# The last stage of a convolution and expert kernel, rearranged image by image

## The chip, the cores and the metric

The kernel runs on one core of a Trainium2 chip. The metric is the device time of one execution in microseconds (us). A core has five engines that run side by side, each through its own queue of instructions in a fixed order: TensorE (PE: matmuls; PEld is its load of the stationary operand), VectorE (DVE), ScalarE (ACT), GpSimd (POOL) and SyncE (SP, which here only starts transfers). Engines wait for one another by semaphores. Matmul results land in PSUM, eight banks of 512 fp32 values in each of 128 partitions; everything else on the core lies in SBUF. All data here are fp32.

## The reference

Layer 0 takes x of 32 images, 128 channels, 56 by 56. It computes a 7 by 7 depthwise convolution, a layer norm over the channels, and a mixture of 8 experts with 2 per token and a limited number of places per expert; the result is `input + x_skip + layer_scale * moe`. Layer 1, which the last stage of the kernel computes, is coordinate attention and a 3 by 3 convolution:

```python
x_h = x.mean(3) + x[..., :w // 2].mean(3) + x[..., :w // 4].mean(3)
x_w = x.mean(2) + x[:, :, :h // 2].mean(2) + x[:, :, :h // 4].mean(2)
y = jnp.concatenate([x_h, x_w], axis=2)
y = jnp.einsum('ncl,mc->nml', y, w1) + b1[None, :, None]       # 128 channels to 8
y = _h_swish(_bn1d(y, g1, be1, m1, v1))
xh, xw = (y[:, :, :h], y[:, :, h:])
a_h = jax.nn.sigmoid(jnp.einsum('nml,cm->ncl', xh, wh) + bh[None, :, None])[:, :, :, None]
a_w = jax.nn.sigmoid(jnp.einsum('nml,cm->ncl', xw, ww) + bw[None, :, None])[:, :, None, :]
out = x * a_w * a_h
out = lax.conv_general_dilated(out, wc, window_strides=(1, 1), padding=[(1, 1), (1, 1)], ...)
out = (out + bc[None, :, None, None]) * s2[None, :, None, None] + (be2 - m2 * s2)[None, :, None, None]
return out * jax.nn.sigmoid(out)
```

## The kernel before

Four stages follow one another: the depthwise convolution, the layer norm and gates, the experts (whose last scatter GpSimd issues up to 3122.7 us), and layer 1. The experts leave two tables of token rows in device memory, `acc_d`: for each token one row that its first expert wrote and one that its later expert wrote. Layer 1 starts from `input + beta + first row + second row`. A row of token data is 137 values, of which 128 are read.

**Stage 4 by pairs.** The loop at the end runs over 16 pairs of images and one more turn. `load_pair` (L945) brings two images of x, 3136 KB, into `x1`. Each pair has seven `combine` steps (L950) of seven tiles of 128 tokens: two transfers of 448 KB bring the rows of both tables (`xn`, `x2`; L955), GpSimd adds them (L958), TensorE turns each tile (L964), and VectorE adds turned rows, beta and x in place, 512 columns at a time (L966). When half an image is complete, `squeeze` (L970) multiplies it by w1, four row groups side by side in the partitions of one PSUM bank (L979), and VectorE sums the result along rows and columns (L981, L982). fp32 matmuls go through TensorE in two passes, so a group of four matmuls shows as eight.

`attend` (L984) follows for a whole image: VectorE scales the sums by `wq` (L989) and adds them (L990), TensorE gathers them (L994, L997), VectorE makes the swish (L1000 to L1002), TensorE multiplies by wh and ww (L1006, L1007), and ScalarE computes both sigmoids from PSUM into SBUF tiles (L1008, L1009). VectorE then multiplies the whole image, 3136 elements per partition, by each of them (L1012, L1013): the gate. The second product goes into `pad`, which has a border of zeros.

**The convolution** works on four output rows at a time, through six combinations of six input rows, so that each needs only three horizontal taps. `attend` also makes the combinations: GpSimd and ScalarE compute `t`, `d` and `v` for the whole image at once (L1020 to L1031). `conv` (L1034) takes half an image (seven groups of four rows): six products `m[k]`, each of three taps of 392 columns into one of five PSUM banks (L1041), that is 36 passes; ScalarE copies one to `odd` (L1046), VectorE makes the first sum and difference (L1047, L1048) and adds the other products in ten steps (L1051), ScalarE applies the batch norm and silu (L1053) and starts the output (L1054). In a pair's turn the four half images of the pair before are convolved between the `combine` steps.

**The order.** The framework plans the order of each engine's instructions while the kernel is built: earlier in the program goes first, but an instruction that its own cost estimates find not yet ready lets ready ones pass. On the chip the order is then fixed. That is why the trace shows matmuls of the squeeze two or four at a time between conv passes. Sequence is also set by buffers: `x1` 2, row tiles 3, `pad` 2, `v` 2, `d` and `t` 1, `y` and `odd` 3, turned tiles 2 banks, products 5 banks, and one bank (`pa`) for the squeeze and all of the attention. The transfers of the rows wait for the 14 small VectorE clears (L854, `fence`) that follow the last scatter. SP's queue holds, in order, the loads of weights and vectors, then x and rows.

Of the kernel before, what the change touches and what calls it, by code (L numbers as in the profile page):

```python
# [38 lines left out]
VB = 2  # L39
# [8 lines left out]
def moe_conv_then_coordatt_kernel(ctx: ExitStack, tc: tile.TileContext, a: dict, out: bass.AP):  # L48
# [809 lines left out]
    with ExitStack() as st:  # L858
        cp1 = st.enter_context(tc.tile_pool(name="cc", bufs=1, reuse_waits="tile"))
        xp = st.enter_context(tc.tile_pool(name="cx", bufs=2, reuse_waits="tile"))  # L860
        kp = st.enter_context(tc.tile_pool(name="ck", bufs=3, reuse_waits="tile"))
        sp = st.enter_context(tc.tile_pool(name="cs", bufs=2, reuse_waits="tile"))
        hp = st.enter_context(tc.tile_pool(name="ch", bufs=1, reuse_waits="tile"))
        op = st.enter_context(tc.tile_pool(name="co", bufs=3, reuse_waits="tile"))
        mp = st.enter_context(tc.tile_pool(name="cm", bufs=3, reuse_waits="tile"))
        vp = st.enter_context(tc.tile_pool(name="cv", bufs=VB, reuse_waits="tile"))
        ptp = st.enter_context(tc.tile_pool(name="cpt", bufs=2, space=PSUM))
        psp = st.enter_context(tc.tile_pool(name="cps", bufs=1, space=PSUM))
        pcp = st.enter_context(tc.tile_pool(name="cpc", bufs=5, space=PSUM))
        MIP = 8  # L870
        GR = H // 4
        RP = 7
        SR = 7
        QP = 32

        def vec(name, n):
            t = cp1.tile([n, 1], F32, name=f"v_{name}")
            nc.sync.dma_start(t, a[name])
            return t

        wc = cp1.tile([C, 3, 3, C], F32, name="wc")
        nc.sync.dma_start(wc.rearrange("c h w o -> c (h w) o"), a["wc"])
        wk = [cp1.tile([C, 3, C], F32, name=f"wk{k}") for k in range(5)] + [wc[:, 2]]
        w0, w1, w2 = (wc[:, k] for k in range(3))
        nc.vector.tensor_tensor(wk[0], w0, w2, ALU.add)
        nc.vector.tensor_tensor(wk[1], wk[0], w1, ALU.add)
        nc.vector.tensor_tensor(wk[2], wk[0], w1, ALU.subtract)
        nc.vector.scalar_tensor_tensor(wk[0], w0, 0.25, w2, ALU.mult, ALU.add)  # L890
        nc.vector.scalar_tensor_tensor(wk[3], w1, 0.5, wk[0], ALU.mult, ALU.add)
        nc.vector.scalar_tensor_tensor(wk[4], w1, -0.5, wk[0], ALU.mult, ALU.add)
        for k in range(1, 5):
            nc.vector.tensor_scalar(wk[k], wk[k], 1.0 / 6.0 if k > 2 else -1.0 / 6.0, None, ALU.mult)
        nc.vector.tensor_scalar(wk[0], w0, 0.25, None, ALU.mult)

        w1t = cp1.tile([C, QP], F32, name="w1t")
        nc.gpsimd.memset(w1t, 0.0)
        nc.sync.dma_start(w1t[:, 0:MIP], a["w1"])

        quarter = [x / 56 for x in (7.0, 3.0, 1.0, 1.0)]
        wq = cp1.tile([P, 4], F32, name="wq")
        for k in range(4):
            nc.gpsimd.memset(wq[:, k : k + 1], quarter[k])
        pick = [ident[:, QP * j : QP * j + MIP] for j in range(4)]
        pick_w = [cp1.tile([P, MIP], F32, name=f"pick_w{k}") for k in range(2)]
        for k in range(2):
            nc.vector.tensor_scalar(pick_w[k], pick[0], quarter[2 * k], None, ALU.mult)
            for j in range(1, 4):
                nc.vector.scalar_tensor_tensor(pick_w[k], pick[j], quarter[2 * k + j // 2], pick_w[k], ALU.mult, ALU.add)  # L910
        wht = cp1.tile([MIP, C], F32, name="wht")
        nc.sync.dma_start(wht, a["wh"])
        wwt = cp1.tile([MIP, C], F32, name="wwt")
        nc.sync.dma_start(wwt, a["ww"])
        for t in (wht, wwt):
            nc.vector.tensor_scalar(t, t, 1.0 / 6.0, None, ALU.mult)
        bh, bw = vec("bh", C), vec("bw", C)

        def folded(g, be, mean, v, b, n):

            vg, vb, vm, vv, vbias = (vec(x, n) for x in (g, be, mean, v, b))
            s = cp1.tile([n, 1], F32, name=f"s_{g}")
            o = cp1.tile([n, 1], F32, name=f"o_{g}")
            mh = cp1.tile([n, 1], F32, name=f"mh_{g}")
            nc.gpsimd.memset(mh, -0.5)
            nc.vector.tensor_scalar(s, vv, 1e-5, None, ALU.add)
            nc.gpsimd.tensor_tensor(s, s, mh, ALU.pow)
            nc.vector.tensor_tensor(s, s, vg, ALU.mult)
            nc.vector.tensor_tensor(o, vbias, vm, ALU.subtract)
            nc.vector.tensor_tensor(o, o, s, ALU.mult)  # L930
            nc.vector.tensor_tensor(o, o, vb, ALU.add)
            return s, o

        s1, o1 = folded("g1", "be1", "m1", "v1", "b1m", MIP)
        s2, o2 = folded("g2", "be2", "m2", "v2", "bc", C)

        pads = []
        for k in range(2):
            t = cp1.tile([C, H + 2, W + 2], F32, name=f"pad{k}")
            nc.gpsimd.memset(t, 0.0)  # L940
            pads.append(t)
        QT = 7
        L = H + W

        def load_pair(i):  # L945
            x1 = xp.tile([C, 2, HW], F32, tag="x1", name=f"x1_{i}")
            nc.sync.dma_start(x1, a["x"][2 * i : 2 * i + 2].rearrange("n c h w -> c n (h w)"))
            return x1

        def combine(i, q, x1):  # L950
            j0 = i * TPP + q * QT
            xn = kp.tile([P, QT, C], F32, tag="cxn", name=f"cxn{i}_{q}")
            x2 = kp.tile([P, QT, C], F32, tag="cx2", name=f"cx2{i}_{q}")
            for t, r0 in ((xn, j0 * P), (x2, T1 + j0 * P)):
                d = nc.sync.dma_start(t, acc_d[r0 : r0 + QT * P, 0:C].rearrange("(j p) c -> p j c", p=P))  # L955
                for x in fence:
                    after(d.ins, x)
            nc.gpsimd.tensor_tensor(xn, xn, x2, ALU.add)  # L958
            xf = x1.rearrange("c n f -> c (n f)")
            for g in range(0, QT, 4):  # L960
                n = min(4, QT - g)
                pt = ptp.tile([C, 4 * P], F32, tag="pt", name=f"cpt{i}_{q}_{g}")
                for j in range(n):
                    nc.tensor.transpose(pt[:, j * P : (j + 1) * P], xn[:, g + j, :], ident)  # L964
                cols = slice((q * QT + g) * P, (q * QT + g + n) * P)
                nc.vector.scalar_tensor_tensor(xf[:, cols], pt[:, 0 : n * P], beta_c, xf[:, cols], ALU.add, ALU.add)  # L966

        sums = {}

        def squeeze(i, im, half, x1):  # L970

            if half == 0:
                sums[i, im] = (psp.tile([P, SR * W + L], F32, tag="pa", name=f"cpa{i}_{im}"),
                               sp.tile([P, 2, SR, 4], F32, tag="rs", name=f"rs{i}_{im}"),
                               sp.tile([P, 2, W], F32, tag="cs", name=f"cs{i}_{im}"))
            pa, rs, cs = sums[i, im]
            for j in range(4):
                f0 = (4 * half + j) * SR * W
                nc.tensor.matmul(pa[j * QP : (j + 1) * QP, 0 : SR * W], lhsT=w1t, rhs=x1[:, im, f0 : f0 + SR * W],  # L979
                                 start=True, stop=True)  # L980
            nc.vector.tensor_reduce(rs[:, half], pa[:, 0 : SR * W].rearrange("p (r q v) -> p r q v", r=SR, q=4), AX.X, ALU.add)  # L981
            nc.vector.tensor_reduce(cs[:, half, :], pa[:, 0 : SR * W].rearrange("p (r w) -> p w r", r=SR), AX.X, ALU.add)  # L982

        def attend(i, im, x1):  # L984
            img = x1[:, im, :].rearrange("c (h w) -> c h w", h=H)
            nm = f"{i}_{im}"
            pa, rs, cs = sums.pop((i, im))
            ry = sp.tile([P, 2, SR], F32, tag="ry", name=f"ry{nm}")
            nc.vector.tensor_tensor(rs, rs, bc(wq.unsqueeze(1).unsqueeze(1), [P, 2, SR, 4]), ALU.mult)  # L989
            nc.vector.tensor_reduce(ry, rs, AX.X, ALU.add)  # L990
            pl = pa[:, SR * W : SR * W + L]
            py = pl[0:MIP, :]
            for j in range(4):
                nc.tensor.matmul(py[:, 0:H].rearrange("m (k j r) -> m k j r", k=2, j=4)[:, :, j, :], lhsT=pick[j], rhs=ry,  # L994
                                 start=True, stop=True)
# [63 lines left out]
        for i in range(NPAIR + 1):  # L1059
# [3 lines left out]
            for q in range(NQ):  # L1063
# [9 lines left out]
                for x in todo[: per_q[q]]:  # L1073
                    conv(*x)
# [61 lines left out]
```

## Time and profile before

| | us |
|---|---|
| time, median of 3 runs (lowest, highest) | 4329.18 (4310.08, 4334.66) |
| the profiled execution's time | 4323.54 |
| its span | 4321.8 |
| stage 4 in the span, from the first setup of it | about 3123 to the end, 1199 |
| PE, DVE, ACT, POOL busy in it | 1079, 971, 361, 934 |

The profile is of one execution; its parts used here are windows (busy time of each engine in a stretch), groups of instructions by line, waits (who waited for whom), the timeline, and the chain of work that ended last. A busy DVE or POOL instruction includes time for which it stood inside the engine and could not move. `PEclk`, the granted TensorE clock, is 1.00 in nearly all of stage 4 after 3300 us and 0.50 to 0.53 between 3123 and 3150.

### The profile page before, as it was taken

What the parts mean: (1) busy time and instruction counts of PE and PEld (TensorE: products, weight loads), DVE (VectorE), ACT (ScalarE), POOL (GpSimd) and SP (SyncE); (2) the same over time, 40 slices, a digit from 0 to 9 for tenths busy, and PEclk for the clock granted to TensorE, in tenths of its full rate; (3) what the DMA queues carried; (4) which work ended last, traced back from release to release, by engine and by line L of the source; (5) the groups of instructions that cost most, each with busy time, mean ns of one, the idle gap of its engine ahead of it and who ended that gap; (6) DMA issues with size and microseconds to landing.
All of it is one profiled execution on the core that took longest, in us unless ns stands there. A gap on an engine that the chain in (4) does not pass through costs nothing. (4 is left out here: it accounts for less than half of the span.)

```text
span 4321.8 us, 60777 instructions
## 1 busy us (share of the span) xinstructions
PE 3526.6 (82%) x21765; PEld 2018.7 (47%) x21765; DVE 2571.0 (59%) x5370; ACT 1447.6 (33%) x3123; POOL 2752.9 (64%) x2044
## 2 busy tenths in 40 slices
PE   7999979884169858778688668989669999999999
PEld 4555559884134434444344334434334444454444
DVE  4333329999748648775622112222268888888886
ACT  0000027664034424334344334545312333333332
POOL 5444414333057777576777467777779877788875
PEclk9999989786579879889799889999879999999999
DMA  9999985553982121111222122222265555555551
GB/s 183 179 186 191 188 179 222 245 239 166 327 267 51 51 61 43 48 44 49 54 56 56 45 59 57 56 56 57 60 226 163 193 182 176 166 192 182 184 163 73
DMA packets 678005, 580.92 MB, mean 134 GB/s; under 512 B 405848, under 2 KB 611184, under 8 KB 667248
## 3 DMA queue, kind: packets, MB, share of 16 engines
q1 hardware_dynamic: 411408, 319.81, 25.7%
q10 hardware_dynamic: 222816, 160.70, 14.1%
q0 software_dynamic: 43264, 94.64, 8.1%
q8 instruction: 187, 3.06, 0.3%
q14 instruction: 330, 2.70, 0.2%
HBM read 314.92 MB, written 260.09 MB: 133 GB/s over the span
## 5 line engine op out<-in xcount | busy, mean ns | idle before, releaser
L702 POOL DMA_INDIRECT acc_d<-yo,row x676 | 685.7, 1014 | 274.9 <-DMA acc_d<-yo,row 70.4
L1041 PE MATMUL pc<-v,wk 128*128 128x392 f32 x1920 | 705.5, 510 | 0.4 <-POOL v L1026 0.4
L661 PE MATMUL ph<-fxt,w 128*128 128x512 f32 (+1 forms) x1400 | 682.5, 631 | 0.5 <-ACT ht L662 0.5
L640 POOL DMA_INDIRECT xg_r<-acc_d,idx x556 | 557.4, 1003 | 183.9 <-issue 108.5
L669 PE MATMUL py<-ht,w 128*128 128x512 f32 (+1 forms) x1400 | 624.6, 589 | 0.0
L165 PE MATMUL acc<-xs,band 28*64 28x432 f32 (+2 forms) x11264 | 536.1, 527 | 51.8 <-issue 33.0
L662 ACT ACTIVATE ht<-ph,bias 128x512 f32<-128x512 f32 (+1 forms) x700 | 476.8, 682 | 248.9 <-PE ph L661 246.4
L1041 PEld LDWEIGHTS pc<-v,wk 128*128 128x128 f32 x1920 | 348.2, 191 | 308.5 <-issue 104.9
L165 PEld LDWEIGHTS acc<-xs,band 28*64 28x64 f32 x11264 | 311.2, 132 | 276.1 <-issue 182.9
L310 PE MATMUL lnps<-proj,lnyt 128*128 128x136 f32 x1568 | 364.7, 401 | 67.4 <-ACT sq L315 38.8
L661 PEld LDWEIGHTS ph<-fxt,w 128*128 128x128 f32 x1400 | 274.1, 207 | 279.3 <-issue 250.9
L310 PEld LDWEIGHTS lnps<-proj,lnyt 128*128 128x128 f32 x1568 | 350.9, 316 | 81.7 <-ACT sq L315 47.9
L669 PEld LDWEIGHTS py<-ht,w 128*128 128x128 f32 x1400 | 254.6, 190 | 261.1 <-issue 259.2
L1051 DVE SCALAR_TENSOR_TENSOR y<-pc,y 128x392 f32<-128x392 f32 x640 | 317.3, 553 | 14.9 <-PE pc L1041 14.9
L1021 POOL TENSOR_TENSOR d<-pad 128x3248 f32<-128x3248 f32 x32 | 228.0, 7125 | 151.8 <-DVE pad L1013 151.8
L958 POOL TENSOR_TENSOR cxn<-cxn,cx 128x896 f32<-128x896 f32 x112 | 267.3, 2395 | 75.6 <-DMA cxn<-acc_d 28.8
L696 DVE TENSOR_TENSOR ys<-pb,xg_r 128x512 f32<-128x512 f32 (+2 forms) x147 | 98.3, 671 | 341.3 <-PE pb L678 341.1
L181 DVE TENSOR_TENSOR yt<-acc,m 128x448 f32<-128x448 f32 x256 | 146.4, 620 | 260.3 <-PE acc L165 188.3
L671 ACT ACTIVATE fyt<-py,b 128x512 f32<-128x512 f32 (+1 forms) x175 | 119.6, 683 | 507.0 <-PE py L669 496.7
L653 DVE COPY fxt<-pt 128x512 f32<-128x512 f32 (+1 forms) x175 | 119.5, 683 | 241.7 <-PE pt L651 238.7
L693 ACT ACTIVATE yo<-xg_r,own 128x137 f32<-128x137 f32 (+1 forms) x568 | 194.3, 404 | 191.1 <-DVE own L689 128.3
L331 DVE SCALAR_TENSOR_TENSOR xn<-cen,rstd,gamma_bc 128x128 f32<-128x128 f32 x784 | 213.5, 340 | 47.2 <-POOL rstd L324 47.2
(243 smaller groups left out, 5035.4 us busy)
## 6 DMA issues: line engine op xcount, KB each, us to landing
acc_d<-xn SPq DMA_DIRECT2D x16, 3356.5 KB
acc_d<-yo ACTq DMA_DIRECT2D x4, 13426.0 KB
lnyt<-y_d SPq DMA_DIRECT2D x16, 3136.0 KB
x<-in_x SPq DMA_DIRECT2D x16, 3136.0 KB
cxn<-acc_d SPq DMA_DIRECT2D x112, 448.0 KB
cx<-acc_d SPq DMA_DIRECT2D x112, 448.0 KB
out<-y ACTq DMA_DIRECT2D x64, 784.0 KB
xt<-in_x ACTq DMA_DIRECT2D x64, 392.0 KB
```

The costliest lines, as they stand in the source:

```text
L165: nc.tensor.matmul(acc[r][half * M : (half + 1) * M, :, lo:hi], lhsT=band[rows, t0 + o - least, 1 - par : 1 - par + M], rhs=xs[i][rows, ha ...
L310: nc.tensor.matmul(ps[:, j, :], lhsT=yf[:, self.j0 + g + j, :], rhs=proj, start=True, stop=True)
L331: nc.vector.scalar_tensor_tensor(pair.row[:, self.j0 + j, 0:C], self.cen[:, j, 0:C], self.rstd[:, j : j + 1], gamma_bc, ALU.mult, ALU.mult)
L640: d = nc.gpsimd.indirect_dma_start(out=xg[0:n, k, :], out_offset=None, in_=acc_d[0:T1, :], in_offset=bass.IndirectOffsetOnAxis(ap=idx[0][0 ...
L661: nc.tensor.matmul(ph[:, 0:N_], lhsT=w[0][:, f * P : (f + 1) * P], rhs=xt[:, 0:N_], start=True, stop=True)
L662: nc.scalar.activation(ht[:, f, 0:N_], ph[:, 0:N_], AF.Gelu, bias=w[2][:, f : f + 1])
L669: nc.tensor.matmul(py[:, 0:N_], lhsT=w2[:, f, :], rhs=ht[:, f, 0:N_], start=(f == 0), stop=(f == NF - 1))
L702: d = nc.gpsimd.indirect_dma_start(out=acc_d[:, :], out_offset=bass.IndirectOffsetOnAxis(ap=row[0:n, k : k + 1], axis=0), in_=yo[0:n, k, : ...
L958: nc.gpsimd.tensor_tensor(xn, xn, x2, ALU.add)
L1021: nc.gpsimd.tensor_tensor(d, high, low, ALU.subtract)
L1041: nc.tensor.matmul(m[k], lhsT=wk[k][:, dw, :], rhs=v[:, k, rows, dw : dw + W], start=(dw == 0), stop=(dw == 2))
L1051: nc.vector.scalar_tensor_tensor(r[x], m[k], f, r[y_], ALU.mult, ALU.add)
```

## The change

Stage 4 goes image by image. Rows come in blocks of eight image rows, seven to an image: 448 tokens as four tiles of 112 (`load_rows`), with x in blocks too (`load_x`), eight blocks ahead. GpSimd adds the second table's rows to the first's (`summed`), four blocks ahead; TensorE turns the four tiles and VectorE writes the merged block straight into the padded image (`merge`), which is gated in place. The sigmoids are written back to PSUM, `wq` is copied there once, and the swish starts from PSUM, so no VectorE step of the loop reads two SBUF tensors. The combinations are made for half an image at a time, in two parts (`combined`); `d`, `t`, `v` and `y` hold half an image. Each image has a slot of pieces in a written order (`slots`): in the first half of slot k the blocks of image k are merged between the conv pieces of the second half of image k-2; in the second half image k is attended and gated between the conv pieces of the first half of image k-1. There are 34 slots. Constants load through ScalarE's queue, and the borders of `pad` alone are cleared, by VectorE. The planner works as before. The setup of the weights is left out here, as it computes the same values.

Of the removed lines, which the listing above has, none is repeated here.

```diff
+    trp = ctx.enter_context(tc.tile_pool(name="ctr", bufs=2, space=PSUM))
+    pcp = ctx.enter_context(tc.tile_pool(name="cpc", bufs=5, space=PSUM))
...
+    MB = 8
+    NM = H // MB
+    MT = 2 * W
+    NX = 8
...
+    xss = [cp1.tile([C, MB, W], F32, name=f"xs{k}") for k in range(NX)]
+    cxs = [[cp1.tile([MT, BLK, C], F32, name=f"cx{i}_{k}") for i in range(2)] for k in range(NX)]
+    def load_x(m):
+        nc.sync.dma_start(xss[m % NX], a["x"][m // NM][:, m % NM * MB : (m % NM + 1) * MB, :])
+    def load_rows(m):
+    ys = [cp1.tile([C, RP, 4, W], F32, name=f"y{k}") for k in range(2)]
+    odd = cp1.tile([C, RP, W], F32, name="odd")
+    pads = [cp1.tile([C, H + 2, W + 2], F32, name=f"pad{k}") for k in range(2)]
+    vs = [cp1.tile([C, 6, RP, W + 2], F32, name=f"v{k}") for k in range(2)]
+    d_t = cp1.tile([C, RP, 4, W + 2], F32, name="d_t")
+    t_t = cp1.tile([C, RP, 2, W + 2], F32, name="t_t")
...
+    pa = psp.tile([P, SR * W + L + 8], F32, name="pa")
...
+    wq_ps = pa[:, SR * W + L : SR * W + L + 4]
+    nc.vector.tensor_copy(wq_ps, wq)
...
+    for t in pads:
+        nc.vector.memset(t[:, 0 : H + 2 : H + 1, :], 0.0)
+        nc.vector.memset(t[:, :, 0 : W + 2 : W + 1], 0.0)
+    def summed(m):
+        if m < NM * N:
+            x, x2 = cxs[m % NX]
+            nc.gpsimd.tensor_tensor(x, x, x2, ALU.add)
+    def merge(k, q):
+        m = NM * k + q
+        pt = trp.tile([P, BLK * P], F32, tag="tr", name=f"cpt{k}_{q}")[:, 0 : BLK * MT]
+        for j in range(BLK):
+            nc.tensor.transpose(pt[:, j * MT : (j + 1) * MT], cxs[m % NX][0][:, j, :], ident[0:MT, 0:MT])
+        nc.vector.scalar_tensor_tensor(pads[k % 2][:, 1 + q * MB : 1 + (q + 1) * MB, 1 : W + 1],
+                                       pt.rearrange("c (r w) -> c r w", w=W), beta_c, xss[m % NX], ALU.add, ALU.add)
+        if m + NX < NM * N:
+            load_x(m + NX)
+            load_rows(m + NX)
+        summed(m + 4)
+    def squeeze(n, half):
+        pad = pads[n % 2]
+        for j in range(4):
+            r0 = 1 + (4 * half + j) * SR
+            nc.tensor.matmul(pa[j * QP : (j + 1) * QP, 0 : SR * W], lhsT=w1t, rhs=pad[:, r0 : r0 + SR, 1 : W + 1],
+                             start=True, stop=True)
+        nc.vector.tensor_reduce(rs[:, half], pa[:, 0 : SR * W].rearrange("p (r q v) -> p r q v", r=SR, q=4), AX.X, ALU.add)
+        nc.vector.tensor_reduce(cs[:, half, :], pa[:, 0 : SR * W].rearrange("p (r w) -> p w r", r=SR), AX.X, ALU.add)
+    pl = pa[:, SR * W : SR * W + L]
+    def pooled(n):
+        nc.vector.tensor_tensor(rs, rs, bc(wq_ps.unsqueeze(1).unsqueeze(1), [P, 2, SR, 4]), ALU.mult)
+        nc.vector.tensor_reduce(ry, rs, AX.X, ALU.add)
+        py = pl[0:MIP, :]
+        for j in range(4):
+            nc.tensor.matmul(py[:, 0:H].rearrange("m (k j r) -> m k j r", k=2, j=4)[:, :, j, :], lhsT=pick[j], rhs=ry,
+                             start=True, stop=True)
         for k in range(2):
+            nc.tensor.matmul(py[:, H:L], lhsT=pick_w[k], rhs=cs[:, k, :], start=(k == 0), stop=(k == 1))
+        nc.vector.tensor_scalar(py, py, s1, o1, ALU.mult, ALU.add)
+        nc.vector.tensor_scalar(r_t, py, 3.0, 0.0, ALU.add, ALU.max)
+        nc.vector.scalar_tensor_tensor(z_t, r_t, 6.0, py, ALU.min, ALU.mult)
+    def attend(n):
+        ph, pw = pl[:, 0:H], pl[:, H:L]
+        nc.tensor.matmul(ph, lhsT=wht, rhs=z_t[:, 0:H], start=True, stop=True)
+        nc.tensor.matmul(pw, lhsT=wwt, rhs=z_t[:, H:L], start=True, stop=True)
+        nc.scalar.activation(ph, ph, AF.Sigmoid, bias=bh)
+        nc.scalar.activation(pw, pw, AF.Sigmoid, bias=bw)
+    def gate(n):
+        img = pads[n % 2][:, 1 : H + 1, 1 : W + 1]
+        nc.vector.tensor_tensor(img, img, bc(pl[:, H:L].unsqueeze(1), [C, H, W]), ALU.mult)
+        nc.vector.tensor_tensor(img, img, bc(pl[:, 0:H].unsqueeze(2), [C, H, W]), ALU.mult)
+    def combined(n, ch, part):
+        v, pad = vs[ch], pads[n % 2]
+        r0 = 4 * RP * ch
+        byq = lambda x: x.rearrange("c (g r) w -> c g r w", r=4)
+        low, high = byq(pad[:, r0 : r0 + 4 * RP, :]), byq(pad[:, r0 + 2 : r0 + 2 + 4 * RP, :])
+        d, t = d_t, t_t
+        if part == 0:
             nc.scalar.mul(t, low[:, :, 1:3, :], 4.0)
             nc.gpsimd.tensor_tensor(d, high, low, ALU.subtract)
             nc.gpsimd.tensor_tensor(t, high[:, :, 1:3, :], t, ALU.subtract)
             nc.gpsimd.tensor_tensor(v[:, 1], t[:, :, 1, :], t[:, :, 0, :], ALU.add)
             nc.gpsimd.tensor_tensor(v[:, 2], t[:, :, 1, :], t[:, :, 0, :], ALU.subtract)
+        else:
+            nc.scalar.mul(v[:, 3], d[:, :, 1, :], 2.0)
+            nc.scalar.mul(d[:, :, 0:2, :], d[:, :, 0:2, :], 4.0)
+            nc.gpsimd.tensor_tensor(v[:, 4], d[:, :, 2, :], v[:, 3], ALU.subtract)
+            nc.gpsimd.tensor_tensor(v[:, 3], d[:, :, 2, :], v[:, 3], ALU.add)
             nc.gpsimd.tensor_tensor(v[:, 0], d[:, :, 2, :], d[:, :, 0, :], ALU.subtract)
             nc.gpsimd.tensor_tensor(v[:, 5], d[:, :, 3, :], d[:, :, 1, :], ALU.subtract)
+    PASSES = {3: ((2, 0, 4.0), (3, 1, 8.0), (0, 0, 1.0), (1, 1, 2.0)),
+              4: ((0, 0, 1.0), (1, 1, -2.0), (2, 2, 4.0), (3, 3, -8.0)), 0: ((0, 0, 1.0),), 5: ((3, 3, 1.0),)}
+    def product(n, ch, k):
+        m = pcp.tile([P, RP, W], F32, tag="pc", name=f"pc{n}_{ch}_{k}")
+        for dw in range(3):
+            nc.tensor.matmul(m, lhsT=wk[k][:, dw, :], rhs=vs[ch][:, k, :, dw : dw + W], start=(dw == 0), stop=(dw == 2))
+        return m
+    def conv(n, ch, ks):
+        y = ys[ch]
+        r = [y[:, :, k, :] for k in range(4)]
+        m = {k: product(n, ch, k) for k in ks}
+        if 1 in m:
             nc.scalar.copy(odd, m[1])
             nc.vector.tensor_tensor(r[0], m[2], odd, ALU.add)
             nc.vector.tensor_tensor(r[1], odd, m[2], ALU.subtract)
+        for k in ks:
+            for x, y_, f in PASSES.get(k, ()):
                 nc.vector.scalar_tensor_tensor(r[x], m[k], f, r[y_], ALU.mult, ALU.add)
+        if 5 in m:
             yf = y.rearrange("c r t w -> c (r t) w")
             nc.scalar.activation(yf, yf, AF.Silu, bias=o2, scale=s2)
+            nc.scalar.dma_start(out[n][:, 4 * ch * RP : 4 * (ch + 1) * RP, :], yf)
+    def slots(k):
+        new = lambda f, *x: (lambda: f(*x)) if k < N else None
+        old = lambda d, f, *x: (lambda: f(k - d, *x)) if 0 <= k - d < N else None
+        cv = lambda *ks: old(2, conv, 1, ks)
+        pieces = [new(merge, k, 0), cv(1, 2), old(1, combined, 0, 1), new(merge, k, 1), new(merge, k, 2), cv(3),
+                  new(merge, k, 3), new(squeeze, k, 0), cv(4), new(merge, k, 4), new(merge, k, 5), cv(0), new(merge, k, 6),
+                  new(squeeze, k, 1), cv(5)]
+        cv = lambda *ks: old(1, conv, 0, ks)
+        pieces += [old(1, combined, 1, 0), new(pooled, k), cv(1, 2), new(attend, k), old(1, combined, 1, 1), cv(3),
+                   new(gate, k), cv(4), cv(0), cv(5), new(combined, k, 0, 0)]
+        return [f for f in pieces if f]
+    for m in range(4):
+        summed(m)
+    for k in range(N + 2):
+        for f in slots(k):
+            f()
```

## The prediction

> **What bounds the kernel now.** The change touches only the last stage, so I read the page's 40 slices first to place it (about 3123 us to the end, 1199 of the 4321.8 us span), then windows of one pair of images each, then the waits of TensorE, then the timeline around one gate. Windows of two steady pairs (columns: length, then busy time of PE, PEld, DVE, ACT, POOL, then granted clock, DMA share, GB/s):
>
> ```profile
> 3867.00:3938.00 71.00, 66.92 (x259) 34.99 (x258) 60.63 (x85) 22.79 (x22) 58.29 (x24) 1.00 0.57 184
> 3938.00:4009.00 71.00, 66.83 (x259) 34.75 (x258) 60.62 (x86) 22.79 (x22) 58.33 (x25) 1.00 0.57 182
> ```
>
> TensorE is idle only 4.1 us per pair, 2.05 us per image; VectorE and GpSimd have 10 and 13 us idle per pair. What TensorE waits for in 3797 to 4080 us (eight images; total, times, longest):
>
> ```profile
> PE cpa L994 <- DVE ry L990: 7.5, 7, 1.2
> PE cpa L1006 <- DVE z L1002: 7.2, 8, 1.0
> ```
>
> Both are small VectorE steps of the attention. The timeline shows the same steps first with GpSimd idle or between instructions, and then in the steady state:
>
> ```profile
> 3157.96 0.21 DVE L989 TENSOR_TENSOR rs<-rs,wq 128x56 f32<-128x56 f32 x1
> 3160.43 0.26 DVE L1002 SCALAR_TENSOR_TENSOR z<-r,z 8x112 f32<-8x112 f32 x1
> 3167.12 3.41 DVE L1013 TENSOR_TENSOR pad<-x,ah 128x3136 f32<-128x3136 f32 x1
> ...
> 3871.31 2.06 DVE L1002 SCALAR_TENSOR_TENSOR z<-r,z 8x112 f32<-8x112 f32 x1
> 3873.29 1.97 DVE L1051 SCALAR_TENSOR_TENSOR y<-pc,y 128x392 f32<-128x392 f32 x4
> 3879.00 4.83 DVE L1013 TENSOR_TENSOR pad<-x,ah 128x3136 f32<-128x3136 f32 x1
> ...
> 3902.97 1.89 DVE L989 TENSOR_TENSOR rs<-rs,wq 128x56 f32<-128x56 f32 x1
> 3911.46 4.39 POOL L958 TENSOR_TENSOR cxn<-cxn,cx 128x896 f32<-128x896 f32 x1 [2.91 <-issue]
> ```
>
> Steps with two SBUF inputs wait for a GpSimd step, and hold one up (4.39 us where it took 2.08 alone). Steps with one input in PSUM (L1051) stay at 0.49 us, and GpSimd's L1021, beside them, at 7.10 to 7.16 us. Period: the gates of image 0 and of image 30 end at 3170.5 and 4237.1 us, 35.55 us per image; an undisturbed pair takes 70.6, 35.3 per image. The end, from the chain of work (start, length):
>
> ```profile
> 4261.56 53.55 PE pc L1041 x162
> 4315.13 0.58 DVE y L1051
> 4315.73 1.69 ACT y L1053
> ```
>
> After the last gate TensorE alone decides (0.331 us per pass), then 4.4 us of output.
>
> **The change part by part, per image.**
>
> *VectorE.* The scaling of the row sums falls from 1.65 (by-form mean) to 0.21, the swish from 1.79 to 0.26, the gate from 3.55 + 4.69 to 3.40 + 3.41. Now: 20 accumulating steps at 0.49 = 9.8, 4 first ones at 0.5 = 2.0, seven merges of 448 elements (512 take 0.635 pipelined, so 0.57) = 4.0, four reductions 2.1, small ones 1.4, gate 6.8: 26.1 us, against 60.6/2 = 30.3. It is not the bound; this frees 4 us that decide nothing by themselves.
>
> *TensorE.* Conv passes are the same 72. Transposes go from 24.5 to 28; seven take 0.77, so 3.5 x 0.11 = +0.4. Squeeze: 16 passes in both, but now all four of a half are issued together. Eight passes in a row took 1.39 us, two alone 0.78; the chain's pieces of one pair add to 8.4, so 4.2 per image now and 2.8 if both halves stay together: -1.4, or 0 where the planner pulls them apart as it does now; I take -0.7. Busy 33.25 - 0.7 + 0.4 = 32.95. The idle 2.05 goes: the picks and the attention's matmuls are now followed or preceded by ready conv pieces (cv(5), cv(1, 2)), and the VectorE step ahead of them is 0.2 and not 1.9 us.
>
> *GpSimd.* 64 differences of 1624 elements (7.12/2 = 3.56) 7.1 per image, the t steps 3.1, v1 and v2 3.3, v3 and v4 3.55, v0 and v5 3.85; the row sums are seven of 512 elements on 112 partitions, 2.08 x 512/896 = 1.19 each = 8.3 (7.3 before, uncontended). With about 0.05 us for each of 12 more instructions: 29.8 us. It was 28.1 uncontended, 29.2 with its stalls. This is 90% of a period of 33; what is late next, if anything, is here.
>
> *The wait that is added.* GpSimd's row sums run only four blocks ahead, and its first-half pieces of image k stand in its queue behind gate(k). From gate(k) to the last row sum of image k+1 GpSimd does difference, t, v1, v2 (6.8), v4, v3, v0, v5 of the half (3.6), three sums (3.6): 14.0. From there to the end of gate(k+1): transposes 0.45, merge 0.57, squeeze 1.4, reductions 1.04, scaling 0.45, picks 0.6, swish 0.9, matmuls 0.6, sigmoids 0.8, gate 6.8 = 13.6, plus 4.7 for the conv products and accumulations that stand ahead on TensorE and VectorE (cv(5) and cv(1, 2) partly) = 18.3. The ring takes 32.3 us, just under TensorE's 32.95. Queued behind gate(k) on VectorE are cv(4), cv(0), cv(5); TensorE has five product banks to run on, 10 us, and the gate takes 6.8. Period: 32.95 + 0.35 for remaining waits = 33.3; ends 31.9 (squeezes together, no wait) and 35.3 (nothing gained).
>
> *ScalarE.* One sigmoid and one swish table load per image as now (8 and 8 in eight images); 11.4 us of work per image, covered by a period of 33.
>
> *Buffers.* y has one per half image (three before): its output must land before cv(1, 2) of that half a slot later, some 16 us after issue; at the end it takes 4.4. odd has one: its two readers run 16 us before the next copy. Sigmoids stay in the bank that the squeeze writes: squeeze(k, 0) waits for gate(k-1), which ends about 3 us into the slot, the squeeze stands 8 us into it. None is on the path.
>
> *Transfers.* SP issues 21 per image instead of 7.5; an issue is 0.36 to 0.52 us, 10 us per image, in a queue that otherwise waits. Bytes are the same 6.4 MB per image: at 182 GB/s 35.2 us, at the 426 GB/s of the busiest window (3923 to 3927) 15. Since DMA is at share 0.57, I take it as hidden; the cover gone, it is the first rival below. The Trainium skill speaks against smaller transfers: SBUF — State Buffer, The DMA setup-cost knee, gives each about 2 us fixed plus bytes at 436 GB/s. One after the other, 21 of 229 KB would be an estimated 53 us per image, and the end at some 4815 us. The rows here show several 448 KB transfers in flight at 316 to 426 GB/s for 12 us on end, so I go by bytes.
>
> *Front.* SP no longer issues 13 small loads ahead of the data (3122.89 to 3128.9), and two 2.9 us clears leave GpSimd. The rows become readable at 3124.8, when VectorE's fence is through. First sum at about 3129.5 (two issues 1.0, 458 KB at 361 GB/s 1.3, 2.3 to land, as the scatters' transfers before it took; it was 3142.66, behind a 3136 KB load), seven sums at 1.27 each (458 KB at 361 GB/s, just over GpSimd's 1.19): 3138.4. With the 13.6 us chain and 3 more for a granted clock that stood at 0.50 there, gate(0) ends at 3155, between 3150 and 3165; now 3170.5. VectorE's set-up, 10 us in 3124.7 to 3136.7 now, ends before the seventh merge. Image 1 has few conv pieces beside it: 29 us (14.0 + 13.6 and little else).
>
> *End.* After gate(31) three half images are left, 36 passes of 0.331 = 11.9 us each, less 2 already begun: 33.7. GpSimd needs 20.8 for both halves of image 31, so TensorE decides. With 0.6 + 1.7 + 4.4: 40.4 us, 39 to 45. Now it is 51.7 (that gate ends at 4270.1).
>
> **Sum.** 3155 + 29 + 30 x 33.3 + 40.4 = 4223.4 us of span, -98.4 against the profiled 4321.8 (15.5 at the front, 71.6 between the first and last gate, 11.3 at the end). That execution took 4323.54, 0.13% under the median of 4329.18; the same difference from the median gives 4231. Own range 4182 (gate(0) at 3150, period 31.9, end 39: 4175 of span) to 4296 (gate(0) at 3165, 35, end 45: 4289).
>
> **Rivals.**
> Transfers: smaller pieces come late, GpSimd's sum stands at the head of its queue waiting for rows, and the period stays at 35.3. For it: the loads bunch in the first half, 4.8 MB in some 16 us, 300 GB/s. Against: 361 and 399 GB/s at the front. 3155 + 29 + 1059 + 40.4 = 4283.4, a time of 4291. Chance 0.10.
> The change doesn't do what it says: PSUM operands don't free the steps. Then 2 us idle stay, period 35.3, again 4291. Against: L1051 and L966, one operand in PSUM, never stretch. Chance 0.06.
> Slower: the ring through GpSimd. If all of cv(5), cv(1, 2), cv(3) and the latter's accumulations come ahead of the gate, the second part is 13.6 + 2.0 + 4.1 + 2.0 + 2.0 = 23.7 and the period 37.7: 4355.4 of span, 4363. It decides from a period of 36.6 (1097.4/30), a second part of 22.6. For it: program order is just this, GpSimd runs at 90%, sums only four blocks ahead, and waits in the middle of its queue for the gate. Against: the planner takes ready work first, as the split squeezes of now show. Chance 0.19, a quarter of it near 36.6, so within 0.5%.
>
> **How the numbers follow.** Forecast 0.65, rivals 0.10, 0.06, 0.19. A measurement here can tell about 0.5%, 22 us. Faster by more: the forecast and most of the first two, 0.77. Within: 0.07. Slower: 0.16. The range holds the forecast's own, both 4291 cases and the ring's lighter half: 4190 to 4340, leaving out about 0.05 below and 0.13 above.
>
> **What would show it.** In steady windows: scaling and swish under 0.4 us, both gate steps near 3.4 in every image, GpSimd's differences near 3.6; sigmoid table loads 33.3 us apart; TensorE busy 32 to 33 of it. Wrong if TensorE's transposes wait for GpSimd's sums by over 3 us per image, if the sums wait for DMA, or if the gate takes more than 7.5 us. The front is right if the first sum starts before 3132, the end if the last sigmoid is 45 to 55 us from the end (gate included).

## The result, and the profile after

The changed kernel takes 4361.81 us (median of 4; 4355.74 to 4375.92), the kernel before beside it 4323.16 (median of 4; 4310.08 to 4334.66): ratio 1.0104, 95% interval 1.0079 to 1.0129. It is slower by 1.0%; 4231 us and a gain of 2.3% were forecast. The profiled execution took 4355.74 with a span of 4354.0. One run further down, of the kernel with PSUM undone, fell in a slower state of the chip and is left out of its median.

The ends of the stage came as forecast, the middle did not. The gate of image 0 ends at 3151.7 us (forecast 3155), image 1 follows after 28.8 (29), and from the end of the last gate, 4314.3, it is 39.8 us to the end (40.4). Between the gates of image 1 and image 31 lie 1133.7 us, 37.8 per image, where 33.3 were forecast and 35.5 had been. 30 x 4.5 = 135 us; less the 3 us by which the front came early, that is the whole error of 131.

Windows of the kernel after (length, then busy time of PE, PEld, DVE, ACT, POOL, then clock, DMA share, GB/s); the third is the last image, when no more rows are to be summed or loaded:

```profile
3870.00:3941.00 71.00, 64.86 (x238) 33.76 (x238) 45.65 (x73) 23.24 (x28) 59.23 (x46) 0.93 0.64 175
3941.00:4012.00 71.00, 65.41 (x242) 33.52 (x241) 45.63 (x80) 22.20 (x27) 59.00 (x46) 0.93 0.60 164
4277.00:4311.00 34.00, 34.00 (x135) 17.66 (x134) 26.02 (x44) 11.79 (x14) 21.72 (x16) 1.00 0.12 48
```

VectorE has lost 15 us of work per 71 us, as the change says. No engine is full, TensorE is idle 6 us in 71 (it was 4), and its clock is at 0.93 where it was 1.00. In the last image it never stops. The waits of 3500 to 4200 us, some 18.5 images (total, times, longest):

```profile
ACT v L1035 <- POOL d_t L1030: 268.4, 35, 11.4
DVE y L1058 <- ACT odd L1057: 77.9, 19, 6.2
POOL cx L971 <- DMA cx<-acc_d: 75.3, 19, 5.3
PE pa L1011 <- DVE z_t L1007: 48.8, 19, 4.7
```

TensorE waits for the swish (L1007), which on VectorE stands behind the first sum of a half image (L1058), which waits for ScalarE's copy `odd`; and GpSimd's row sums (L971) wait for rows. The chain of work joins these. One turn of it (start, length; the pieces between are left out where "..." stands):

```profile
3888.86 0.38 ACT odd L1057
...
3889.26 0.57 DVE y L1058
...
3890.81 0.27 DVE z_t L1007
...
3891.12 0.67 PE pa L1011 x2
3891.79 0.43 PE pa L1012 x2
3892.22 8.15 PE pc L1048 x18
3900.36 0.40 PE cpt L977 x4
...
3901.80 1.28 POOL cx L971
3903.10 0.33 SPq L886
...
3903.52 3.14 DMA cx<-acc_d
...
3906.80 1.26 POOL cx L971
3908.06 3.59 POOL d_t L1030
...
3920.01 3.63 POOL d_t L1030
...
3923.66 0.55 ACT v L1035
...
3925.03 1.68 ACT y L1065
3926.71 0.38 ACT odd L1057
```

From `odd` to the next `odd` it is 37.85 us, the period. The gate is not in this chain: it ended at 3901.4 and GpSimd began the difference `d` of the gated image only at 3908.0. GpSimd's own timeline shows why:

```profile
3901.80 1.27 POOL L971 TENSOR_TENSOR cx<-cx,cx 112x512 f32<-112x512 f32 x1 [3.83 <-issue]
3906.79 1.27 POOL L971 TENSOR_TENSOR cx<-cx,cx 112x512 f32<-112x512 f32 x1 [3.72 <-DMA cx<-acc_d]
3908.02 3.63 POOL L1030 TENSOR_TENSOR d_t<-pad 128x1624 f32<-128x1624 f32 x1
```

Two sums stand ahead of `d` and wait 3.8 us each for rows. They are the sums of blocks of the image after next, some 35 us ahead of the transposes that need them. The program writes a sum four blocks ahead; the planner, which lets ready work pass, had moved it ahead, in front of `d`; by its rule it must have held the rows to be there and `d` to be still waiting for the gate.

SP's queue has a part in these waits that is easily overlooked. A load of the second table waits for the sum that frees its buffer, and every load behind it in SP's queue waits too. In the chain above the rows for the second sum leave right after such a load, which SP could issue only when the first sum was done (3903.10). SP's waits of 3500 to 4200:

```profile
SPq L886 <- POOL cx L971: 513.8, 110, 10.1
```

How much of the loss is due to SP's order alone was not tested.

### The profile page after: what moved, and what is told of

Its sections match the earlier page's. It is cut to its first block, busy times and chain, and to the rows that moved or that the text cites. A ratio compares the mean times of both kernels' runs of the same rounds, so it can differ in the third digit from the quotient of the medians.

```text
span 4354.0 us, 62611 instructions
## 1 busy us (share of the span) xinstructions
PE 3584.1 (82%) x21877; PEld 2046.6 (47%) x21877; DVE 2432.2 (56%) x5381; ACT 1458.1 (33%) x3219; POOL 2779.6 (64%) x2405
## 5 line engine op out<-in xcount | busy, mean ns | idle before, releaser
L1048 PE MATMUL pc<-v,wk 128*128 128x392 f32 x2304 | 884.0, 525 | 5.8 <-POOL v L1032 4.8
L702 POOL DMA_INDIRECT acc_d<-yo,row x676 | 685.1, 1014 | 265.9 <-issue 80.5
L1048 PEld LDWEIGHTS pc<-v,wk 128*128 128x128 f32 x2304 | 431.2, 199 | 361.6 <-issue 133.7
L971 POOL TENSOR_TENSOR cx<-cx,cx 112x512 f32<-112x512 f32 x224 | 284.0, 1274 | 231.7 <-DMA cx<-acc_d 131.1
L1030 POOL TENSOR_TENSOR d_t<-pad 128x1624 f32<-128x1624 f32 x64 | 232.4, 3632 | 15.9 <-DVE pad L1019 15.7
```

The costliest lines, as they stand in the source:

```text
L702: d = nc.gpsimd.indirect_dma_start(out=acc_d[:, :], out_offset=bass.IndirectOffsetOnAxis(ap=row[0:n, k : k + 1], axis=0), in_=yo[0:n, k, : ...
L971: nc.gpsimd.tensor_tensor(x, x, x2, ALU.add)
L1030: nc.gpsimd.tensor_tensor(d, high, low, ALU.subtract)
L1048: nc.tensor.matmul(m, lhsT=wk[k][:, dw, :], rhs=vs[ch][:, k, :, dw : dw + W], start=(dw == 0), stop=(dw == 2))
```

## Experiments

Chips differ: on some, the stages ahead of this one take 560 us more. So each run has its difference (of the medians) to the kernel before, on the same chip and in the same rounds, its ratio with a 95% interval, which is not the quotient of these medians, and the period, from gate to gate, from its own profile. A ring is a closed chain of waits through several engines, from a step of one image to the same step of the next; the longest ring sets the period. The changed kernel, run once more so, is 33.5 us above before (ratio 1.0081, 1.0044 to 1.0118), where 40 to 50 were expected.

> The changed kernel again, on the chip of the runs below, so that they can be set against it and not only against the kernel before: 40 to 50 us above before, 38 us from gate to gate.

**Sums where they are written.** An ordering edge on GpSimd's queue, that waits for nothing (`behind`), keeps each sum behind `last`, the last step of a `combined` part written ahead of it.

```diff
-            nc.gpsimd.tensor_tensor(x, x, x2, ALU.add)
+            s = nc.gpsimd.tensor_tensor(x, x, x2, ALU.add)
+            if last:
+                behind(s.ins, last[0])
...
```

> The change as it is, but GpSimd's row sums stay behind the combination steps ahead of which the program writes them (ordering edges on GpSimd's own queue, no new wait). Theory A, GpSimd's queue closes the ring: in the changed kernel two sums stand ahead of the difference d of the gated image and wait 3.8 us each for rows; here d starts within 1 us of the gate's end (it was 6.6 us), and the 36 to 38 us from gate to gate become 33.5 to 34.5: 28 images x 4 us less than 4362, so 4250, between 4230 and 4290. Theory B, ScalarE's queue closes it (the copy odd stands behind v3 of the second half): under 1% less, 4320 to 4362. Theory C, the ring written in the prediction (conv products and accumulations ahead of the gate): no change, 4340 to 4365.

+46.8 us, ratio 1.0096 (1.0058 to 1.0134): no gain, theory A fails as it was put. The two waits are gone, `d` starts 0.1 us after the gate, yet the period stays, 37.65 us, the same in nearly every image. GpSimd and ScalarE of this run:

```profile
4437.90 3.64 POOL L1038 TENSOR_TENSOR d_t<-pad 128x1624 f32<-128x1624 f32 x1 [7.25 <-DVE pad L1027]
...
4449.93 7.41 POOL L977 TENSOR_TENSOR cx<-cx,cx 112x512 f32<-112x512 f32 x6
4457.31 3.61 POOL L1038 TENSOR_TENSOR d_t<-pad 128x1624 f32<-128x1624 f32 x1
```

```profile
4460.95 0.54 ACT L1043 ACTIVATE v<-d_t 128x406 f32<-128x406 f32 x1 [14.14 <-POOL d_t L1038]
...
4462.32 1.68 ACT L1073 ACTIVATE y<-y,o_g,s_g 128x1568 f32<-128x1568 f32 x1
4463.90 0.46 ACT L1065 COPY odd<-pc 128x392 f32<-128x392 f32 x1
```

Seven sums, six of them in a row, now lie between the two `d` of an image, and ScalarE stands 14.14 us at the head of its queue with `v3 = 2 d1` of the second half, with the silu and `odd` behind it. From the gate's end (4437.8) over `d`, sums, `d`, `v3`, silu, `odd`, swish, sigmoids to the next gate's end (4475.4): 37.65 us. The work that was ahead of the gate is behind it, in the same ring.

**The copy `odd` on VectorE.**

```diff
-            nc.scalar.copy(odd, m[1])
+            nc.vector.tensor_copy(odd, m[1])
```

> The change as it is, but VectorE makes the copy odd of the first product, not ScalarE. Theory B: VectorE's wait for odd, 77.9 us in 19 images (4.1 each), goes, the swish behind it comes as much earlier, TensorE's wait for z (about 5 us per image) goes, and the period falls from 38 to 34: 4362 - 28 x 4 = 4250, between 4230 and 4290. Theory A: the link through ScalarE is only one of the ring's, d still stands behind two sums that wait for rows; under 1.5% less, 4300 to 4362. Theory C: no change.

+47.7 us, ratio 1.0093 (1.0068 to 1.0118), period about 38: no gain here either; VectorE's wait for `odd` and TensorE's for the swish are gone, but GpSimd waits 62.1 us in 16 sums for rows, 3.9 each, and the sigmoids stand behind the start of an output, which waits for a transfer of rows.

**Both edits.**

> Both edits, sums in their written order and the copy odd on VectorE. A and B: TensorE's own work decides, 33 to 33.7 us per image: 3152 + 29 + 30 x 33.4 + 40 = 4223, between 4205 and 4250. Theory C: 4330 to 4365.

-35.0 us, ratio 0.9924 (0.9900 to 0.9948), period 34.59: together they gain 82 us over either alone, but miss the number. The chain of this run, of GpSimd and ScalarE alone between two gates:

```profile
4415.00 0.90 POOL d_t L1038
...
4427.05 2.79 POOL cx L977 x3
...
4430.70 2.49 POOL cx L977 x2
4433.18 3.58 POOL d_t L1038
...
4436.79 0.55 ACT v L1043
...
4438.15 1.69 ACT y L1073
...
4440.28 1.28 ACT L1021
```

The swish is no longer behind `v3`, but the sigmoids (L1021) still are, and the sums are between the two `d`.

**Sums six ahead.** As the run before, with the sums written six blocks ahead.

```diff
-        summed(m + 4)
+        summed(m + 6)
...
```

> Row sums in written order, but written six blocks ahead and not four, and the copy odd on VectorE. With four ahead the period was 34.59 with GpSimd busy from the gate's end to the last sum: that is the ring of the prediction (gate, combinations, sums, transposes, squeeze, gate). If so, two more sums ahead take 2.5 us out of it and TensorE decides: 33.0 to 33.9 us per image, and the first gap falls from 34.0 to about 29: 25 to 50 us below the run with four ahead, 60 to 85 below before. If it is TensorE itself that needs 34.6 (finer pieces, 33.9 us busy): the period stays, only the first gap gains, 5 us. If sums at six ahead wait for rows: over 34.6.

-75.4 us, ratio 0.9827 (0.9791 to 0.9863), period 33.69. Windows of the two (with four ahead, then with six):

```profile
4400.00:4700.00 300.00, 293.69 (x1150) 151.98 (x1146) 236.63 (x385) 97.64 (x108) 260.64 (x199) 1.00 0.70 183
```

```profile
3600.00:4000.00 400.00, 400.00 (x1570) 208.46 (x1570) 320.44 (x525) 128.95 (x143) 358.58 (x272) 1.00 0.73 191
```

The number came, not for the reason given: the ring at 34.59 was not the prediction's (sums, transposes, squeeze), but the one in the chain above. Of the five sums ahead of the second `d` three stay (3.71 us), `d` and `v3` come earlier, and TensorE works without a pause, through transfers at 191 GB/s. What stays is TensorE's own work, 33.69 us.

**The order alone.** `odd` stays on ScalarE, and `v3` of the second half is put behind it (`copied`, the latest one) in ScalarE's queue; sums six ahead.

```diff
-            nc.scalar.mul(v[:, 3], d[:, :, 1, :], 2.0)
+            twice = nc.scalar.mul(v[:, 3], d[:, :, 1, :], 2.0)
+            if ch == 1:
+                behind(twice.ins, copied[0])
...
```

> As the run before with sums six ahead, but the copy odd stays on ScalarE, and v3 of the second half is put behind it in ScalarE's queue: no work changes its engine, only the order. If the place in the queue was the matter and not the work: within 15 us of the run with odd on VectorE, a period under 34.5. If ScalarE's work itself is the matter, or if v3 behind odd comes too late for GpSimd: 36 to 38 us per image, 70 us or more above it.

-93.8 us, ratio 0.9805 (0.9753 to 0.9857), period 33.69; a second time, on another occasion, -80.5 (0.9853, 0.9819 to 0.9887). TensorE works without a pause here too:

```profile
3600.00:4000.00 400.00, 400.00 (x1570) 207.85 (x1569) 305.96 (x502) 139.27 (x168) 359.50 (x272) 1.00 0.68 193
```

No work has left its engine: the places of the sums and of `v3` in two queues were the whole loss of the change, and what it was to gain comes out. This version beats both kernels. Two parts of it were not run by themselves: sums six ahead without the move of `v3`, and that move with the sums four ahead.

> The repaired order once more, on the chip of the other three runs: 33.69 us per image, 85 to 100 us below before.

**No sums.** The row sums are left out; the second table's rows are loaded, but are missing from the result.

```diff
-            nc.gpsimd.tensor_tensor(x, x, x2, ALU.add)
+            pass
```

> The changed kernel without GpSimd's row sums (the second table's rows are loaded, but left out of the result). Two rings of nearly one length (one through ScalarE's queue, 37.65 us in the run with the sums in written order, one through sums that wait for rows, 38 us in the run with odd on VectorE), both through GpSimd: both lose the sums, 7.4 us of GpSimd's work between d of the first half and d of the second, and the waits for rows. Then TensorE decides: 33 to 34 us per image, 4.3 x 29 = 125 us below the changed kernel, 70 to 90 below before. Rival, the ring through ScalarE does not hold the sums: 36 to 38 us stay, at most 50 below the changed kernel.

-48.9 us (0.9882, 0.9837 to 0.9926), less than the 70 to 90 that were expected. From image 12 on 33.74 us, with TensorE full; images 3 to 11 take 34 to 40. In these the loads of the second table, which nothing holds up any more, run far ahead (DMA share 1.17, 270 GB/s from 3280 to 3500, later 0.46). So the expectation on the sums holds where the transfers are quiet; the run also takes a quarter of the traffic out there (143 GB/s, against 191 in the run with six ahead), and doesn't tell sums from transfers. The run with six ahead does, as it has all of both.

**Which wait for rows closes the second ring.** Two places were left open: the two sums ahead of `d`, and the start of the output ahead of the sigmoids. The start is put behind the sigmoids, once with `odd` on VectorE, once in the changed kernel as it is.

```diff
-            nc.scalar.dma_start(out[n][:, 4 * ch * RP : 4 * (ch + 1) * RP, :], yf)
+            start = lambda: nc.scalar.dma_start(out[n][:, 4 * ch * RP : 4 * (ch + 1) * RP, :], yf)
+            if ch == 1 and n + 2 < N:
+                held.append(start)
+            else:
+                start()
...
-        nc.scalar.activation(pw, pw, AF.Sigmoid, bias=bw)
+        sig = nc.scalar.activation(pw, pw, AF.Sigmoid, bias=bw)
+        while held:
+            tc.add_manual_dep(held.pop()().ins, sig.ins.name,
+                              mybir.DependencyInfo(mybir.DependencyClass.NoSync, mybir.DependencyReason.DATA),
+                              reason="the output starts behind the sigmoids")
```

> The run with odd on VectorE (38 us per image, sums where the planner put them), and the start of the second half's output is put behind the sigmoids in ScalarE's queue. If that start, which waits for a transfer of rows with the sigmoids behind it, closes the second ring: the period falls from 38 to 34.5 or less, 4381 less 28 x 3.6 = 4280, 50 to 75 us below before. If the two sums ahead of d, 3.8 us of wait each, close it: 37 to 38 stays, 30 to 50 above before. If both: 35 to 37.

+59.6 us (1.0127, 1.0087 to 1.0166), period 38.7, a little above the 37 to 38 that were expected if the two sums decide: the start of the output is not what does. The chain of waits of this run goes round through the sums:

```profile
4454.51 3.34 DVE pad L1025
4457.85 0.34 SPq L881
...
4458.29 4.59 DMA cx<-acc_d
...
4462.92 0.09 issue
4463.01 1.28 POOL cx L971
4464.31 0.33 SPq L886
...
4464.73 3.38 DMA cx<-acc_d
...
4468.25 1.26 POOL cx L971
4469.51 3.58 POOL d_t L1036
```

After the gate SP issues a load of x that had been waiting in its queue, then the rows behind it; they arrive 4.6 us later, the sum, another load, 3.4 us, the second sum, and only then `d`: 11.6 us between the end of the gate and the beginning of `d`, with no work on GpSimd but 2.5 us of sums.

> The changed kernel with that edit alone (odd stays on ScalarE). The ring through odd was 37.65 without any wait for rows, so it stays: 37.5 to 38.3 us per image, within 20 us of the changed kernel. If the start of the output alone made the loss: 34.5, 100 us below it.

+70.2 us (1.0157, 1.0111 to 1.0203), 39 to 40 us per image: no gain, as expected, and a little worse than that.

**The operands in PSUM alone,** in the kernel before: sigmoids, `wq` and the swish's input in the squeeze's bank, which is one tile for all images; nothing else.

```diff
-            nc.vector.tensor_tensor(rs, rs, bc(wq.unsqueeze(1).unsqueeze(1), [P, 2, SR, 4]), ALU.mult)
+            nc.vector.tensor_tensor(rs, rs, bc(wq_ps.unsqueeze(1).unsqueeze(1), [P, 2, SR, 4]), ALU.mult)
...
-            nc.vector.scalar_tensor_tensor(z, r, 6.0, z, ALU.min, ALU.mult)
+            nc.vector.scalar_tensor_tensor(z, r, 6.0, py, ALU.min, ALU.mult)
...
-            nc.scalar.activation(ah, ph, AF.Sigmoid, bias=bh)
+            nc.scalar.activation(ph, ph, AF.Sigmoid, bias=bh)
...
-            nc.vector.tensor_tensor(img, img, bc(aw.unsqueeze(1), [C, H, W]), ALU.mult)
+            nc.vector.tensor_tensor(img, img, bc(pw.unsqueeze(1), [C, H, W]), ALU.mult)
```

> The kernel before with one part of the change alone: sigmoids, scaling weights and swish in PSUM, so that its VectorE steps there have one SBUF input. If those slow steps alone made TensorE's 2.05 us idle per image: the gate takes 3.4 + 3.4, scaling and swish under 0.3, 4323 - 31 x 2 = 4261, between 4250 and 4290. If another wait takes their place (GpSimd's or a transfer's): within 0.5% of 4323.

-73.2 us (0.9834, 0.9792 to 0.9876), and -88.4 (0.9846, 0.9787 to 0.9905) the second time. Two gates take 66.04 us, 33.02 per image, where it was 35.3. Windows and VectorE's groups of it (mean ns of one):

```profile
4400.00:4700.00 300.00, 300.00 (x1162) 157.92 (x1162) 231.93 (x381) 103.14 (x100) 253.84 (x106) 1.00 0.59 190
```

```profile
L1014 DVE TENSOR_TENSOR pad<-x,pa 128x3136 f32<-128x3136 f32 x9 | 30.7, 3412 | 0.0
...
L992 DVE TENSOR_TENSOR rs<-rs,pa 128x56 f32<-128x56 f32 x9 | 1.8, 203 | 0.0
```

Steps with two SBUF inputs were all that TensorE was waiting for, and no new wait took their place. The run frees the gate along with the two small steps. That it was the scaling and the swish rests on the waits before: those behind them were 14.7 us of some 16 that TensorE was idle in eight images.

> The kernel before with the operands in PSUM alone, on the same chip: 33.0 us per image, 65 to 80 us below before. It should stand 10 to 30 us above the repaired order, which has the earlier front (25 us) and the shorter end (10 us) and pays 0.67 us more per image on TensorE (20 us).

On that chip the two good versions are level (4256.55 and, for the repaired order, 4264.43; their intervals overlap). The expected distance didn't show in the medians, the profiled spans are 4244.2 and 4239.6.

**PSUM undone in the repaired order.** Sigmoids, `wq` and the swish go back to SBUF: the lines of the last diff, the other way round, in `pooled`, `attend` and `gate`.

> The repaired order, but the sigmoids, the scaling weights and the swish in SBUF as in the kernel before: the one part of the change that gained by itself is undone. If the steps with two SBUF inputs wait for GpSimd also here: scaling and swish 1.7 to 1.9 us instead of 0.2, the gate 8.2 instead of 6.8, 4.5 us more between the squeeze and d; GpSimd is idle only 3.2 us ahead of d, so 1.3 us and more per image come through: 33.69 to 35 or 36, 40 to 75 us above. If the order has slack for it: within 15 us.

+94.1 us (1.0296, 1.0205 to 1.0386), 175 above the repaired order: more than twice the larger of the expected losses. Gates lie mostly 35 to 45 us apart. One line of VectorE and one of GpSimd:

```profile
3967.94 10.06 DVE L1007 TENSOR_TENSOR rs<-rs,wq 128x56 f32<-128x56 f32 x1
...
3984.58 4.30 POOL L1051 TENSOR_TENSOR v<-d_t 128x406 f32<-128x406 f32 x1 [5.61 <-ACT d_t L1048]
```

The scaling of 56 elements, 0.20 us with `wq` in PSUM, takes 10.06: GpSimd works without a gap from 3962.7 to 3977.9, and the step gets through at 3978.0. In the other direction GpSimd's 1.05 us step takes 4.30 beside the gate. The mean scaling there is 4.49 us.

**Squeezes together,** in the repaired order: the four matmuls of a squeeze behind one another, that of the last rows first.

```diff
-        for j in range(4):
+        one = None
+        for j in (3, 0, 1, 2):
...
+            if one is not None:
+                behind(s.ins, one)
+            one = s.ins
```

> The repaired order of the run with sums six ahead and odd ahead of v3, and the four matmuls of each squeeze kept together behind the merge they all need (ordering edges on TensorE). There TensorE is busy all of the 33.69 us of an image, 4.67 of them from the starts of squeeze matmuls to the next start, as they go two passes at a time. The prediction's term: together they take 2.8, so 33.69 - 1.9 = 31.8 if TensorE alone decides; GpSimd has 30.2 of work and its ring little left, so 32.0 to 33.0: 20 to 55 us below that run. Rival: the squeeze comes later, and the attention behind it, so that the ring through the gate closes again at 33.7 or more: within 10 us or above.

-30.8 us (0.9948, 0.9920 to 0.9977), about 50 slower than the repaired order; period 35.5. TensorE's work does fall: busy 87.27 in 100 us, so 31.0 per image, and the last gap, without sums, is 30.73. But with the new order a load of rows (6.53 us) and six sums (7.37) stand ahead of `d` again, with `v3`, then the sigmoids behind it on ScalarE. The rival of that run was right.

## Why the prediction was wrong

*Scaling, swish, gate:* right. 0.20, 0.26, 3.42 and 3.41 us in every image. That this is what TensorE's idle time comes from was right too: alone it gains 73 to 88 us. The rival "the change doesn't do what it says" is out.

*VectorE, GpSimd:* right in size. In 71 us of the changed kernel VectorE is busy 45.6, 24.3 per image (forecast 26.1), GpSimd 59.2, 31.5 per image (29.8); a sum takes 1.27 us, a `d` 3.63.

*TensorE:* too low. The term was 32.95 + 0.35; without a wait it takes 33.69. From the starts of matmuls to the next start, the kernel before with PSUM operands needs 24.87 for conv passes, 2.86 for transposes and 4.19 for squeezes; the repaired order 24.87, 3.07 and 4.67. Squeezes were to gain 0.7 and lost 0.5, transposes cost 0.2 and not 0.4. With 33.69 and nothing else wrong, the time would have been about 4243.

*The wait that is added:* the step that failed first. The ring's first part was 14.0 us with three sums in it, on the ground that the sums run "four blocks ahead". They don't: the order within GpSimd's queue is the planner's, which put two sums in front of `d`, with their transfers in front of them: 6.6 us from the gate to `d`, instead of none. The sentence "the planner takes ready work first" was used against the slow rival; it is what put them there. The ring as it was written never closed: with the sums held four ahead the third one was done 14.6 us after the gate (forecast 14.0), and the turn was set elsewhere.

*ScalarE:* the step that failed next. "11.4 us of work per image, covered" counts busy time and not places: `odd` stood behind `v3` of the second half, that waits for GpSimd, and the swish behind `odd`; with `odd` gone, the sigmoids behind `v3`. All that GpSimd does up to its second `d`, six sums in one run, is in that ring. Either ring alone gives 37.65 to 38.7; that is why one repair shows nothing. TensorE's clock adds to it: in five images (3862.9 to 4053.8) TensorE is busy 178.28 us, 35.66 each, and idle 2.52; so of 38.18, 1.97 are slower passes and 2.52 waits.

*Buffers* and *Transfers:* "none is on the path" and "hidden" were wrong in the changed kernel, where rows are in the chain between two sums, and right in the repaired order. Bytes are not the matter, since the same traffic flows at 191 GB/s with TensorE full. It is the place of the waiting sum. On the knee that the prediction weighed (the Trainium skill, SBUF — State Buffer, The DMA setup-cost knee), going by bytes was right: 21 transfers per image fit into 33.69 us, not into the 53 estimated from its figures.

*Rivals:* the slow one named 4363 us for a period of 37.7, and 4362 for 37.8 came, but not its mechanism (conv products ahead of the gate). In the changed kernel the chain runs through `odd` and the sums; 18 conv passes are in it, but behind the swish, and the gate is not. With `v3` and the sums moved the period falls to 33.69 with the conv pieces where they were. Its size was luck. The transfers rival had what is seen at GpSimd, a sum that stands at the head of its queue and waits for rows, but laid it to the bunching of the smaller loads and priced it at a period of 35.3. In the repaired order the same loads come and no sum waits for rows (3700 to 4000 us).

## What to carry to other kernels

Price a wait by what stands behind it in that engine's queue, for every engine that the loop passes through, and not by busy shares: here ScalarE was busy a third of the time and closed the ring. A planner that lets ready work pass moves a step ahead of another that it believes late; if the step waits for a transfer on the chip, an ordering edge puts it back. Such an edge adds no wait for another engine, but it can move work into another ring: alone it gained nothing here. When two rings have nearly one length, repair both before judging either.

## What was not expected of the hardware

A VectorE step with two SBUF inputs waited not for one GpSimd step but for a whole unbroken row of them, 10.06 us for 0.20 of work (the longest of the eight scalings in 3700 to 4000 us of the kernel with PSUM undone). The Trainium skill, SBUF — State Buffer, section Who interferes with whom, says that an engine that has the shared ports keeps them for one instruction; here the waiting step let seven whole GpSimd steps pass, until the first gap between two of them.

Short pauses cost TensorE speed afterwards. In 3500 to 4200 us of the changed kernel, the 18 conv passes that follow a wait for the swish of 1.45 to 4.66 us (15 cases) take 7.6 to 9.0 us; after a wait of at most 1.21 us (four cases) they take 6.2:

```profile
3891.12 0.67 PE L1011 MATMUL pa<-z_t,wht 8*128 8x56 f32 x2 [4.58 <-DVE z_t L1007]
...
3892.15 8.22 PE L1048 MATMUL pc<-v,wk 128*128 128x392 f32 x18
```

The granted clock is 0.75 in the 18 passes shown, and 1.00 in those that start at 3853.31, after 1.12 us of wait. The Trainium skill, TensorE: Matmul & The Clock Gate, Part 1, has the clock fall after an idle window of about 3.4 us; here it fell during or just after 11 waits shorter than that. In the kernel before it did so at one of three waits for the swish of 2.2 to 2.5 us (3300 to 4200 us), so the length of one wait alone doesn't decide it.
